# A two-layer graph network on one core: b2's row added by GpSimd, and the node matrix as one float32r product

## The chip, the cores and the metric

The kernel runs on one core of one Trainium2 chip. The metric is the device time of one execution in microseconds (us), the median over several runs. All times below are in microseconds unless marked ns. The engines are called by the profile's names: PE (TensorE, matrix products), DVE (VectorE), ACT (ScalarE), POOL (GpSimd), SP (SyncE, which issues most of the DMAs).

## What is computed

There are 128 independent graphs of 128 nodes with 512 features each, and a dense adjacency matrix per graph. The reference, cut down:

```python
h = relu(layernorm(x))
# layer 0: two hypergraph convolutions
def hypergraph_conv(x, adj, W, b):
    H = (adj != 0)
    w = adj[:, 0, :]                        # first row, weight of each hyperedge
    xw = einsum('ncd,hd->nch', x, W)
    Dn = 1 / einsum('nce,ne->nc', H, w)     # 0 where the sum is 0
    Be = 1 / H.sum(axis=1)
    m = Be[:, :, None] * einsum('nce,nch->neh', H, xw)
    return Dn[:, :, None] * einsum('nce,neh->nch', H, m) + b
t = relu(hypergraph_conv(h, adj, W1, b1))   # 512 -> 1024
t = layer_norm(t, gamma, beta)
x = x + hypergraph_conv(t, adj, W2, b2) + h # 1024 -> 512
# layer 1
h = relu(layernorm(x))
deg = adj.sum(-1)
agg = einsum('bij,bjf->bif', adj, h) / maximum(deg, 1e-6)
x = x + relu(concat([h, agg]) @ W.T)        # 1024 -> 512
```

The two products with H in one convolution are one matrix per graph, S = H diag(Be) H^T, and the sum for Dn is one more column beside it. That matrix is called the node matrix below.

## The kernel before

**Tiling.** One graph is one tile: 128 nodes on the 128 partitions, features along the free axis. All weights stay in SBUF. The products with weights are exact to float32 by a split: each operand is held as a high part, a low part and a third combination of both, all in float32r, and a product is high x high + low x low into one PSUM bank (names ending in m: rm, gm, bm, am) and the third parts into another (rd, gd, bd, ad). So a product of 128 x 512 by 512 x 512 is twelve matrix instructions of 512 columns. The helper `product` issues them; its lines in the profile are L489 (the m bank) and L494 (the d bank).

**Stages and order.** The program is written as small functions, one stage of one graph each, and the order in which they are called is the order of each engine's queue: nothing is reordered later. `step(s)` is called for s from 3 to 124 and holds one call of each stage, for graphs s-4 to s+3 (a software pipeline); `head()` loads and splits the weights and starts the first graphs, `tail()` finishes the last. `steady(g)` is true for graphs 3 to 120; for these conv2's node product (L701 to L703) is split too, and the sum of x, h and b2 is made differently (below).

**What the change touches.**

- `incidence(g)`: a transpose of the adjacency (adjt, L385), the weight column (L387), the test for non-zero with its count (L389), the count's floor and reciprocal (L391, L392), all on DVE. `incidence_scale` multiplies adjt by the reciprocal, on POOL in `step` (L303, tile sb).
- `node_matrix(g)`: one float32 product of adjt with the 129 columns of sb (L404, tile ps_s), and a copy by ACT to SBUF (L406, tile s). float32 products appear as two records each.
- `node_scale(g)`: five small DVE operations in a row on 128x1 tiles (L415 to L420, tile dinv).
- `mean_operator(g)`: a row sum, its floor and its reciprocal on DVE (L339 to L341, tile deg); `mean_scale` scales the adjacency by it, on ACT in `step` (L301).
- `residual(g)`: POOL adds h to x in two halves of 256 columns (L81, tile x_t); then, for steady graphs, `moved` adds b2's row with an accumulating DMA from SBUF to SBUF, issued by POOL (L91). For other graphs POOL adds it, in two more halves.
- `layer1_low(g)`: the low part of layer 1's transposed input (tile hl, L81), on DVE in `step`.
- `combine` splits what POOL does into halves of 256 columns; on DVE it is one instruction of full width. conv1_bias (tile r), conv2_bias (tile g) and residual (x_t) are POOL's additions in `step`.
- `shifts(s - 2, 3)`: a product of two 128x1 columns for a norm, on POOL in `step` (L303, tile st).

Two activations make round trips through DRAM for a transpose: n (inner_out, inner_in, inner_turn with the transpose L550 to nt) and h (layer1_trip_out, layer1_trip_in, layer1_turn, L550 to ht). The adjacency makes one too (mean_out, mean_in, mean_transpose). SP issues all of these.

Of the kernel before, what the change touches and what calls it, by code (L numbers as in the profile page):

```python
# [7 lines left out]
FP = mybir.dt.float32  # L8
FR = mybir.dt.float32r
# [15 lines left out]
def gnn_kernel(  # L25
# [64 lines left out]
    def moved(t, src):  # L90
        nc.gpsimd.dma_start(out=t, in_=src, accum_op=ADD)  # L91

# [66 lines left out]
    b1_bc = const.tile([P, DH], FP, name="b1_bc")  # L159
    b2_bc = const.tile([P, D], FP, name="b2_bc")  # L160
    c0 = const.tile([P, D], FP, name="c0")
# [130 lines left out]
    @stage  # L292
    def load_adjb(g, queue=nc.sync):
        ADJB[g] = pool.tile([P, P], FP, tag="adjb", name="adjb", bufs=2)
        load_blocks(ADJB[g], adj[g], queue)
# [36 lines left out]
    SB, HT, S, DN, H0, Z, PZ, SPLIT = ({} for _ in range(8))  # L332

    @stage
    def mean_operator(g):

        a = ADJ.pop(g)
        deg = small.tile([P, 1], FP, tag="deg", name="deg", bufs=2)
        nc.vector.tensor_reduce(deg, a, AX.X, ADD)  # L339
        nc.vector.tensor_scalar(deg, deg, EPS_DEG, 1.0 / 4096.0, MAX, MUL)  # L340
        nc.vector.reciprocal(deg, deg)  # L341
        ADJ[g] = a, deg
# [37 lines left out]
    @stage  # L380
    def incidence(g):


        HT[g] = at = pool.tile([P, P], FP, tag="ht", name="adjt")
        nc.vector.transpose(at, ADJB.pop(g))  # L385
        SB[g] = sb = small.tile([P, P + 1], FP, tag="sb", name="sb")
        nc.vector.tensor_scalar(sb[:, P : P + 1], at[:, 0:1], DOWN_12, None, MUL)  # L387
        cnt = small.tile([P, 1], FP, tag="cnt", name="cnt", bufs=2)
        nc.vector.tensor_scalar(at, at, 0.0, None, ALU.not_equal, ADD, accum_out=cnt)  # L389

        nc.vector.tensor_scalar(cnt, cnt, 1.0, None, MAX)  # L391
        nc.vector.reciprocal(cnt, cnt)  # L392
        SB[g] = sb, cnt

    @stage
    def incidence_scale(g, eng):
        SB[g], cnt = SB[g]
        scaled(eng, SB[g][:, :P], HT[g], cnt)


    @stage
    def node_matrix(g):
        ps = small_bank("ps_s")
        nc.tensor.matmul(ps[:, : P + 1], HT.pop(g), SB.pop(g), start=True, stop=True)  # L404
        s = small.tile([P, P + 1], FP, tag="s", name="s", bufs=4)
        copy(s, ps[:, : P + 1], AF.Copy, scale=4096.0 if steady(g) else 1.0)  # L406
        S[g] = s[:, :P]
# [3 lines left out]
    def node_scale(g):  # L411
        w = DN[g]
        DN[g] = dn = small.tile([P, 4], FP, tag="dinv", name="dinv", bufs=6)
        inv = dn[:, 2:3]
        nc.vector.tensor_scalar(inv, w, TINY, None, MAX)  # L415
        nc.vector.reciprocal(inv, inv)
        nc.vector.scalar_tensor_tensor(dn[:, 0:1], w, 0.0, inv, ALU.is_gt, MUL)
        nc.vector.tensor_scalar(dn[:, 1:2], dn[:, 0:1], ONE_UP, None, MUL)
        if not steady(g):
            nc.vector.tensor_scalar(dn[:, 3:4], dn[:, 0:1], DOWN_12, None, MUL)  # L420
# [15 lines left out]
    def residual(g, eng=nc.gpsimd):  # L436
        combine(eng, X[g], X[g], H0[g], ADD)
        if steady(g):
            moved(X[g], b2_bc)
        else:  # L440
            combine(eng, X[g], X[g], b2_bc, ADD)
# [373 lines left out]
    def step(s):  # L815
        node_high(s - 2)
        layer1_high(s - 3)
        conv2_bias(s - 2)
        inner_out(s - 1)
        inner_in(s - 1)  # L820
        conv2_high(s - 2)
        node_rest(s - 2)
        node_matrix(s + 1)
        mean_out(s - 3)
        layer1_low(s - 3, nc.vector)
        layer1_self_main(s - 4)
        conv1_weights(s, 1)
        mean_in(s - 3)
        conv2_low(s - 2, nc.vector)
        layer1_self_out(s - 4)  # L830
        conv2_rest(s - 2)
        conv2_nodes(s - 2)
        finish(s - 4)
        load_adj(s - 2)
        layer1_rest(s - 3)
        x_norm(s + 1)
        conv1_main(s, 0)
        conv2_out(s - 2)
        store(s - 4)
        conv1_nodes(s + 1)  # L840
        conv1_main(s, 1)
        conv1_out(s, 1)
        conv1_out(s, 0)
        conv1_high(s + 1)
        conv1_bias(s, 1)
        layer1_mean(s - 3)
        inner_turn(s - 1)
        layer1_sums(s - 2)
        conv1_bias(s, 0)
        conv1_low(s + 1)  # L850
        layer1_self(s - 3)
        layer1_mean_main(s - 3)
        layer1_spread(s - 2)
        load_adjb(s + 3)
        inner_high(s - 1)
        scales(s - 2, 3)
        mean_transpose(s - 3)
        shifts(s - 2, 3, nc.gpsimd)
        layer1_norm(s - 2)
        inner_sums(s)  # L860
        layer1_mean_out(s - 3)
        layer1_mean_high(s - 3)
        inner_low(s - 1, nc.vector)
        mean_rest(s - 3)
        inner_rest(s - 1)
        layer1_mean_low(s - 3, nc.vector)
        layer1_mean_rest(s - 3)
        inner_spread(s)
        scales(s, 2)
        shifts(s, 2, nc.gpsimd)  # L870
        conv2_weights(s - 1)
        layer1_trip_out(s - 2)
        residual(s + 1)
        incidence(s + 2)
        inner_norm(s)
        aggregate(s - 3)
        node_scale(s + 1)
        load_x(s + 2)
        mean_operator(s - 2)
        conv2_main(s - 1)  # L880
        layer1_trip_in(s - 2)
        conv2_weights_out(s - 1)
        x_sums(s + 2)
        x_spread(s + 2)
        mean_scale(s - 2, nc.scalar)
        conv1_rest(s + 1)
        layer1_turn(s - 2)
        incidence_scale(s + 2, nc.gpsimd)
        conv1_weights(s + 1, 0)
        scales(s + 2, 1)  # L890
        shifts(s + 2, 1, nc.vector)

    def head():
        load_w1(0, 0)
        load_x(0)
        load_adjb(0, nc.scalar)
# [547 lines left out]
```

## Time and profile before

| | |
|---|---|
| median of 3 runs | 2458.73 (2458.61 to 2459.32) |
| the profiled execution's own time | 2458.89 |
| its span in the trace | 2457.1 |
| PE busy | 2437.2 (99%) |
| DVE busy | 2340.8 (95%) |
| ACT busy | 2061.8 (84%) |
| POOL busy | 1016.1 (41%) |
| granted PE clock | 1.0 |
| mean DMA rate | 139 GB/s |
| moved by the accumulating DMAs (queue q0) | 30.95 MB in 118 issues, 7.2% of the 16 DMA engines |

Busy time is the union of the spans of an engine's instructions. PE's spans are modelled and overlap, so the cost of one product is read from the distance of two starts, not from its length. The same goes for DVE: an instruction of 0.69 in a row of others starts its follower after 0.61. Spans on POOL are rough. A group's "idle before" is the time in which its engine did nothing just ahead of it, with the one that ended it.

### The profile page before, as it was taken

The page shows a single profiled execution, that of the slowest core. Times are in us where ns is not written, and L with a number is a line of the kernel's source. Part 1 is how long each engine was busy: PE and PEld are TensorE (multiplying, and loading weights), DVE is VectorE, ACT ScalarE, POOL GpSimd, SP SyncE. Part 2 cuts the span into 40 slices and gives each one's busy share as a digit, 9 for nine tenths or more (in the row PEclk, how much of TensorE's full clock was granted, in tenths as well). Part 3 has the DMA queues.
Part 4 walks back from the last instruction along what each step waited for, and adds up shares of the span by engine and source line. Part 5 has one row for each costly group of instructions (what it writes and reads, how often), then busy time and mean ns, then how long its engine had stood idle before and what let it go on. Part 6 is the DMA issues. An engine that isn't in the chain of part 4 may idle for free.

```text
span 2457.1 us, 41143 instructions
## 1 busy us (share of the span) xinstructions
PE 2437.2 (99%) x11300; PEld 2023.8 (82%) x11300; DVE 2340.8 (95%) x5358; ACT 2061.8 (84%) x4494; POOL 1016.1 (41%) x1560
## 2 busy tenths in 40 slices
PE   8999999999999999999999999999999999999998
PEld 6788888888888888888888888888888888888886
DVE  8899999999999999999999999999999999999987
ACT  8888888888888888888888888888888888888885
POOL 5434343444344434443444434343434343434452
PEclk9999999999999999999999999999999999999999
DMA  7454554445444544454455444544554454445432
GB/s 193 132 139 136 141 143 139 136 142 146 136 137 140 149 135 138 139 150 132 139 144 145 136 138 142 143 136 138 144 141 137 138 146 139 136 138 145 127 121 94
DMA packets 425943, 342.30 MB, mean 139 GB/s; under 512 B 178544, under 2 KB 341872, under 8 KB 425712
## 3 DMA queue, kind: packets, MB, share of 16 engines
q1 hardware_dynamic: 407888, 308.66, 41.0%
q0 software_dynamic: 17248, 30.95, 7.2%
q8 instruction: 89, 1.46, 0.3%
q14 instruction: 142, 1.16, 0.2%
q10 hardware_dynamic: 576, 0.07, 0.0%
HBM read 166.21 MB, written 142.34 MB: 126 GB/s over the span
## 4 chain that ended last, share of the span: by engine, by line
PE 83%; DVE 12%; issue 2%; ACT 2%; DMA 1%; SPq 0%; POOL 0%; DVEq 0%; ACTq 0%; POOLq 0%
PE gm L489 16%; PE rm L489 16%; PE bm L489 8%; PE am L489 8%; PE gd L494 8%; PE rd L494 8%; PE bd L494 4%; PE ad L494 4%; PE pz L447 4%; PE am L791 2%; PE ad L791 1%; DVE r L514 1%; PE ps_s L404 1%; PE yd L703 1%; PE ym L701 1%
## 5 line engine op out<-in xcount | busy, mean ns | idle before, releaser
L81 POOL TENSOR_TENSOR r<-r,b_bc 128x256 f32<-128x256 f32 x500 | 355.5, 743 | 772.5 <-DVE r L514 481.4
L303 POOL TENSOR_SCALAR st<-st 128x1 f32<-128x1 f32 x252 | 76.1, 302 | 566.9 <-DVE st L320 566.9
L460 ACT ACTIVATE z<-pz 128x512 fp32r<-128x512 f32 x128 | 76.5, 598 | 206.3 <-PE pz L447 206.3
L329 ACT ACTIVATE r<-r,st 128x1024 f32<-128x1024 f32 x128 | 159.3, 1244 | 76.7 <-POOL st L303 76.6
L81 POOL TENSOR_TENSOR g<-g,c 128x256 f32<-128x256 f32 x246 | 211.1, 1019 | 3.8 <-DVE g L653 3.8
L329 ACT ACTIVATE h<-x_t,st 128x512 f32<-128x512 f32 x255 | 206.2, 809 | 1.1 <-DVE st L303 0.4
L81 POOL TENSOR_TENSOR x_t<-x_t,h 128x256 f32<-128x256 f32 x256 | 184.7, 742 | 5.8 <-ACT h L329 5.8
L314 ACT ACTIVATE h<-x_t,st 128x512 f32<-128x512 f32 x255 | 183.5, 720 | 4.1
L514 DVE SCALAR_TENSOR_TENSOR r<-rd,dinv,r 128x512 f32<-128x512 f32 x256 | 179.8, 742 | 3.7 <-ACT r L509 1.8
L309 ACT ACTIVATE h<-x_t 128x512 f32<-128x512 f32 x255 | 159.5, 626 | 8.4 <-DVE x_t L713 5.5
L509 ACT ACTIVATE r<-rm,dinv 128x512 f32<-128x512 f32 x256 | 162.2, 690 | 4.2 <-PE rm L489 4.1
L550 DVE STREAM_TRANSPOSE nt<-nb 128x1024 f32<-128x1024 f32 x127 | 156.8, 1235 | 2.5 <-DMA nb<-n_scratch 2.5
L580 DVE SCALAR_TENSOR_TENSOR nd<-nh,nl 128x1024 fp32r<-128x1024 f32 x127 | 154.8, 1219 | 0.0
L81 DVE TENSOR_TENSOR nl<-nt,nh 128x1024 fp32r<-128x1024 f32 x126 | 152.2, 1208 | 0.0
L489 PE MATMUL rm<-w11h,z 128*128 128x512 f32 x512 | 152.0, 418 | 0.0
L489 PE MATMUL bm<-w30h,hh 128*128 128x512 f32 x504 | 146.9, 413 | 0.1
L447 PEld LDWEIGHTS pz<-s,h 128*128 128x128 f32 x1024 | 134.4, 192 | 13.7 <-ACT s L406 1.8
L314 ACT ACTIVATE junk<-r,st 128x1024 bf16<-128x1024 f32 x128 | 145.1, 1134 | 0.1
L489 PE MATMUL rm<-w11l,z 128*128 128x512 f32 x512 | 138.2, 392 | 0.0
L494 PE MATMUL rd<-w11d,z 128*128 128x512 f32 x512 | 138.0, 391 | 0.0
L447 PE MATMUL pz<-s,h 128*128 128x128 f32 x1024 | 135.9, 276 | 1.9 <-ACT s L406 1.3
L489 PE MATMUL rm<-w10h,z 128*128 128x512 f32 x512 | 137.7, 391 | 0.0
(240 smaller groups left out, 7527.0 us busy)
## 6 DMA issues: line engine op xcount, KB each, us to landing
n_scratch<-r SPq DMA_DIRECT2D x128, 512.0 KB, 2.6
nb<-n_scratch SPq DMA_DIRECT2D x508, 128.0 KB, 2.8
x_t<-in_x_dram SPq DMA_DIRECT2D x128, 256.0 KB, 2.8
h_scratch<-h SPq DMA_DIRECT2D x127, 256.0 KB, 2.0
hb<-h_scratch SPq DMA_DIRECT2D x508, 64.0 KB, 2.0
out_dram<-o SPq DMA_DIRECT2D x127, 256.0 KB, 2.1
x_t<-b_bc POOLq DMA_DIRECT2D x118, 256.0 KB, 3.7
adj_t<-in_adj_dram SPq DMA_DIRECT2D x128, 64.0 KB, 2.0
```

Of the source, the lines that this page charges most:

```text
L81: eng.tensor_tensor(dst[:, s], a[:, s], b[:, s], op)
L309: copy(junk, src, func, accum_out=t[:, 0:1])
L314: copy(junk, src, AF.Square, bias=t[:, 1:2], accum_out=t[:, 2:3])
L329: copy(dst, src, func, bias=t[:, 5:6], scale=t[:, 4:5])
L447: nc.tensor.matmul(z[:, k * P : (k + 1) * P], H0[g][:, k * P : (k + 1) * P], S[g], start=True, stop=True)
L460: copy(h, pz, AF.Copy, scale=DOWN)
L489: nc.tensor.matmul(pm, left[i](k), right(i, k), start=(i == 0 and k == 0), stop=(i == 1 and k == kk - 1))
L494: nc.tensor.matmul(pd, left[2](k), right(2, k), start=(k == 0), stop=(k == kk - 1), skip_group_check=True)
L509: copy(R[g][:, HALVES[half]], PY.pop((g, half)), AF.Copy, scale=DN[g][:, 1:2])
L514: nc.vector.scalar_tensor_tensor(r, PR.pop((g, half)), dn[:, 0:1], r, MUL, ADD)
L550: nc.vector.transpose(nt.rearrange("p k (i b) -> p k i b", b=B), t.rearrange("p i k a -> p k i a"))
L580: nc.vector.scalar_tensor_tensor(t, h, 2.0**-12, low, MUL, SUB)
```

## The change

`moved` and the accumulating DMAs are gone: a new stage `residual_bias` adds b2's row on POOL, for all graphs. The scaled adjacency is split into high and low by splitting the two scalars alone (`incidence_high`), so that the node matrix is one float32r product of 258 columns, high part and low part side by side; `node_sum` adds the two halves on DVE after ACT has copied the first. The small operations of incidence, node_scale and mean_operator become stages of their own, and are called apart from each other. The order of `step`, `head` and `tail` is new. The diff, cut to its core:

```diff
-    def moved(t, src):
-        nc.gpsimd.dma_start(out=t, in_=src, accum_op=ADD)
...
-        ADJB[g] = pool.tile([P, P], FP, tag="adjb", name="adjb", bufs=2)
+        ADJB[g] = pool.tile([P, P], FP, tag="adjb", name="adjb")
...
     def mean_operator(g):
         nc.vector.tensor_reduce(deg, a, AX.X, ADD)
-        nc.vector.tensor_scalar(deg, deg, EPS_DEG, 1.0 / 4096.0, MAX, MUL)
-        nc.vector.reciprocal(deg, deg)
+    def mean_degree(g, eng):
+        eng.tensor_scalar(deg, deg, EPS_DEG, 1.0 / 4096.0, MAX, MUL)
+    def mean_inverse(g):
+        nc.vector.reciprocal(deg, deg)
...
     def incidence(g):
-        HT[g] = at = pool.tile([P, P], FP, tag="ht", name="adjt")
-        nc.vector.transpose(at, ADJB.pop(g))
-        SB[g] = sb = small.tile([P, P + 1], FP, tag="sb", name="sb")
-        nc.vector.tensor_scalar(sb[:, P : P + 1], at[:, 0:1], DOWN_12, None, MUL)
-        nc.vector.tensor_scalar(at, at, 0.0, None, ALU.not_equal, ADD, accum_out=cnt)
-        nc.vector.tensor_scalar(cnt, cnt, 1.0, None, MAX)
-        nc.vector.reciprocal(cnt, cnt)
+        raw = pool.tile([P, P], FP, tag="ant", name="raw")
+        nc.vector.transpose(raw, ADJB.pop(g))
+        HT[g] = at = pool.tile([P, P], FP, tag="ht", name="adjt").bitcast(FR)
+        two = small.tile([P, 2], FP, tag="cnt", name="cnt", bufs=2)
+        nc.vector.tensor_scalar(at, raw, 0.0, None, ALU.not_equal, ADD, accum_out=two[:, 1:2])
+    def incidence_weight(g, eng):
+        scaled(eng, two[:, 0:1], raw[:, 0:1], DOWN_12)
+    def incidence_count(g, eng):
+        eng.tensor_scalar(two[:, 1:2], two[:, 1:2], 1.0, None, MAX)
+    def incidence_inverse(g):
+        nc.vector.reciprocal(two[:, 1:2], two[:, 1:2])
+    def incidence_high(g):
+        t = small.tile([P, 2 * P + 4], FP, tag="sb", name="sb")
+        SB[g] = sb = t.bitcast(FR)
+        h, l = sb[:, P : 2 * P + 3 : P + 2], sb[:, 2 * P + 1 : 2 * P + 4 : 2]
+        copy(h, two, AF.Copy, scale=DOWN)
+        nc.vector.tensor_tensor(l, two, h, SUB)
+        SPLIT["sb", g] = t[:, 2 * P + 2 : 2 * P + 3], t[:, 2 * P + 3 : 2 * P + 4]
-    def incidence_scale(g, eng):
-        scaled(eng, SB[g][:, :P], HT[g], cnt)
+    def incidence_scale(g, i, eng):
+        scaled(eng, SB[g][:, i * (P + 1) : i * (P + 1) + P], HT[g], SPLIT["sb", g][i])
...
     def node_matrix(g):
-        nc.tensor.matmul(ps[:, : P + 1], HT.pop(g), SB.pop(g), start=True, stop=True)
+        nc.tensor.matmul(ps[:, : 2 * P + 2], HT.pop(g), SB.pop(g)[:, : 2 * P + 2], start=True, stop=True)
         copy(s, ps[:, : P + 1], AF.Copy, scale=4096.0 if steady(g) else 1.0)
+    def node_sum(g):
+        nc.vector.scalar_tensor_tensor(s, PS.pop(g)[:, P + 1 : 2 * P + 2], 4096.0 if steady(g) else 1.0, s, MUL, ADD)
-    def node_scale(g):
-        nc.vector.tensor_scalar(inv, w, TINY, None, MAX)
-        nc.vector.reciprocal(inv, inv)
-        nc.vector.scalar_tensor_tensor(dn[:, 0:1], w, 0.0, inv, ALU.is_gt, MUL)
-        nc.vector.tensor_scalar(dn[:, 1:2], dn[:, 0:1], ONE_UP, None, MUL)
+    def node_floor(g, eng):
+        eng.tensor_scalar(dn[:, 2:3], w, TINY, None, MAX)
+    def node_scale(g):
+        nc.vector.reciprocal(dn[:, 2:3], dn[:, 2:3])
+        nc.vector.scalar_tensor_tensor(dn[:, 0:1], w, 0.0, dn[:, 2:3], ALU.is_gt, MUL)
+    def node_up(g, eng):
+        scaled(eng, dn[:, 1:2], dn[:, 0:1], ONE_UP)
...
     def residual(g, eng=nc.gpsimd):
         combine(eng, X[g], X[g], H0[g], ADD)
-        if steady(g):
-            moved(X[g], b2_bc)
-        else:
-            combine(eng, X[g], X[g], b2_bc, ADD)
+    def residual_bias(g, eng=nc.gpsimd):
+        combine(eng, X[g], X[g], b2_bc, ADD)
```

The new step, in full, since its order is the order of the queues:

```python
def step(s):
    node_high(s - 2); conv2_bias(s - 2); conv2_high(s - 2); layer1_self_main(s - 4)
    layer1_high(s - 3); inner_out(s - 1); conv2_low(s - 2, nc.vector); x_norm(s + 1)
    node_rest(s - 2); conv1_main(s, 0); layer1_self_out(s - 4); conv2_rest(s - 2)
    node_matrix(s + 1); conv1_weights(s, 1); conv1_out(s, 0); mean_out(s - 3)
    layer1_low(s - 3); layer1_rest(s - 3); inner_in(s - 1); conv2_nodes(s - 2)
    node_sum(s + 1); node_floor(s + 1, nc.gpsimd); conv2_out(s - 2); conv1_main(s, 1)
    conv1_out(s, 1); inner_turn(s - 1); layer1_sums(s - 2); mean_in(s - 3)
    layer1_spread(s - 2); conv1_bias(s, 0); load_adj(s - 2); incidence(s + 2)
    layer1_mean(s - 3); incidence_weight(s + 2, nc.vector); scales(s - 2, 3); layer1_mean_main(s - 3)
    finish(s - 4); conv1_bias(s, 1); shifts(s - 2, 3, nc.vector); conv1_nodes(s + 1)
    store(s - 4); load_x(s + 2); inner_high(s - 1); conv1_high(s + 1)
    mean_transpose(s - 3); layer1_mean_out(s - 3); layer1_self(s - 3); mean_operator(s - 2)
    inner_low(s - 1, nc.vector); inner_rest(s - 1); layer1_norm(s - 2); inner_sums(s)
    layer1_mean_high(s - 3); inner_spread(s); conv2_weights(s - 1); layer1_mean_low(s - 3, nc.vector)
    node_scale(s + 1); mean_rest(s - 3); layer1_trip_out(s - 2); x_sums(s + 2)
    incidence_count(s + 2, nc.vector); mean_degree(s - 2, nc.vector); conv2_main(s - 1); scales(s, 2)
    layer1_mean_rest(s - 3); layer1_trip_in(s - 2); conv1_low(s + 1); incidence_inverse(s + 2)
    residual(s + 1); mean_inverse(s - 2); conv2_weights_out(s - 1); conv1_rest(s + 1)
    shifts(s, 2, nc.gpsimd); load_adjb(s + 3); inner_norm(s); incidence_high(s + 2)
    layer1_turn(s - 2); x_spread(s + 2); aggregate(s - 3); mean_scale(s - 2, nc.vector)
    incidence_scale(s + 2, 0, nc.vector); scales(s + 2, 1); conv1_weights(s + 1, 0)
    incidence_scale(s + 2, 1, nc.vector); shifts(s + 2, 1, nc.vector); residual_bias(s + 1); node_up(s + 1, nc.vector)
```

In `head` the weights' loads and splits come in another order: both high parts of w10 and both of w11 are called ahead of conv1_high(0), and incidence_high(0) after w10's; incidence_scale(0, 0) is on POOL.

## The prediction

> **What bounds the kernel now.** I read the page from the top. Busy shares first, then the chain that ended last, then who PE waited for.
>
> ```profile
> PE 2437.2 (99%) x11300; PEld 2023.8 (82%) x11300; DVE 2340.8 (95%) x5358; ACT 2061.8 (84%) x4494; POOL 1016.1 (41%) x1560
> ...
> PE 83%; DVE 12%; issue 2%; ACT 2%; DMA 1%; SPq 0%; POOL 0%; DVEq 0%; ACTq 0%; POOLq 0%
> ```
>
> PE carries the chain, DVE stands close behind. In the list of PE's waits the longest is one of 7.7 us in the start-up; all others together are under 8 us:
>
> ```profile
> PE ps_s L404 <- DVE sb L303: 7.7, 1, 7.7
> ```
>
> So outside the start-up the time is the PE list itself. One step of it, from PE's timeline (start, length, group):
>
> ```profile
> 1212.11 1.07 PE L494 MATMUL gd<-w21d,nd 128*128 128x512 f32 x4
> ...
> 1215.51 1.07 PE L494 MATMUL rd<-w10d,z 128*128 128x512 f32 x4
> 1216.42 0.38 PE L404 MATMUL ps_s<-sb,adjt 128*128 128x129 f32 x2
> 1216.56 1.18 PE L489 MATMUL rm<-w11h,z 128*128 128x512 f32 x4
> 1217.57 1.08 PE L489 MATMUL rm<-w11l,z 128*128 128x512 f32 x4
> ```
>
> The spans overlap, so starts are read. Four products take 0.907 (1216.42-1215.51), one 0.227. From ps_s to 1217.57 is 1.15; less 0.907, the node matrix costs 0.24. A step holds 78 products (17.68), the eight short pz (0.90 in the same way) and ps_s: 18.82; the next ps_s comes 18.86 later. Between 100 and 2350 us PE is busy 2249.7 of 2250: 119 such steps.
>
> DVE's list is as long: its 42 instructions of a step follow each other without a hole. But some of it is waiting inside an instruction:
>
> ```profile
> 1212.28 0.17 DVE L416 RECIPROCAL dinv<-dinv 128x1 f32<-128x1 f32 x1
> 1212.48 0.39 DVE L417 SCALAR_TENSOR_TENSOR dinv<-s,dinv 128x1 f32<-128x1 f32 x1
> 1212.90 0.15 DVE L418 TENSOR_SCALAR dinv<-dinv 128x1 f32<-128x1 f32 x1
> ...
> 1215.77 0.51 DVE L682 SCALAR_TENSOR_TENSOR sp<-sp,s 128x128 fp32r<-128x128 f32 x1
> ```
>
> L417 takes 0.16 elsewhere (in the start-up), L682's twin L683 0.28. Both stand beside an addition of GpSimd, and end as it ends (1212.85, 1216.12):
>
> ```profile
> 1211.42 1.43 POOL L81 TENSOR_TENSOR x_t<-x_t,h 128x256 f32<-128x256 f32 x2
> 1213.15 0.90 POOL L91 DMA_DIRECT2D x_t<-b_bc  x1 [0.30 <-DVE dinv L418]
> 1213.81 0.91 POOL L303 TENSOR_SCALAR sb<-adjt,cnt 128x128 f32<-128x128 f32 x1
> 1214.39 1.73 POOL L81 TENSOR_TENSOR g<-g,c 128x256 f32<-128x256 f32 x2
> ```
>
> **What the Trainium skill says.** (1) SBUF — State Buffer, "Who interferes with whom": a DVE instruction with two SBUF inputs, or in a two-port mode, and a GpSimd instruction that reads SBUF exclude each other; the later waits the whole instruction. The trace agrees: 0.23 at L417, 0.26 at L682. (2) VectorE: DVE Perf Modes, "What auto-detection actually checks": a one-source SBUF operation in float32 can take that two-port mode, so the moved scalings may block too; no view here shows that. (3) TensorE: Matmul & The Clock Gate, "Back-to-back issue gap": N/2.4+2.5 ns, 216 for 512 columns; the trace has 227, so 11 more. (4) DMA: Bandwidth & Descriptors, "Rules for kernel authors": an accumulating DMA must come from GpSimd; here the one such queue is q0, 7.2% of the DMA engines.
>
> **The change part by part, per step.**
> *PE.* One float32r product of 258 columns for two float32 records of 129. By rate (213 of the 227 ns are columns at 2.4 per ns) 258/2.4+13 = 0.121. Gain 0.24-0.12 = **0.12**. Bounds: 0.11 (the skill's formula) to 0.45, if the width were charged at the float32 rate (0.24 x 2); I take 0.12, since every float32r row shows one rate. 119 steps: -14.5 us.
> *DVE, start to start.* Gone: layer1_low (0.60, to POOL), the floor of dinv (0.17). Added: three 128x128 scalings, 0.287 long by the start-up's (9.03 0.29 DVE L303), 0.20 start to start: +0.60; one shift +0.13; node_sum, 129 columns from PSUM, worked out from L514[...]: +0.26; the small low part of incidence_high +0.08. Sum +0.30. Small operations that now stand apart from what they read: L416 to L417 takes 0.20 where an independent one takes 0.08; eight such pairs become three: -0.58. The two port waits above go (-0.49). New port waits, from laying out the new order: finish meets residual's first half on POOL (0.30), the low part meets conv2_bias's first half (0.18), layer1_rest waits for POOL's layer1_low (0.1). 18.86+0.30-0.58-0.49+0.58 = **18.67**, less the short waits on ACT that are in the 18.86 (L320 starts its follower after 0.17, where 0.08 is its own): 18.6. PE's new step is 18.74, so PE stays the bound, by about 0.1. Behind layer1_rest's wait stand node_sum and conv2_out; POOL's node_floor and ACT's layer1_sums wait for those, none of them on PE's path within the next 3 us.
> *POOL.* Off: DMA issue 0.65, scaling 0.6, one shift 0.24. On: residual_bias and layer1_low, four halves of 0.70, floor 0.24. 7.9 busy becomes 9.4 of 18.7. Queued behind its waits: node_floor waits for node_sum, and conv1_bias behind it; conv1_bias feeds inner_sums, which then has 3 us before its result is read. Hidden, since PE reads nothing from POOL within its step but the h low part, 1.6 us later.
> *ACT.* Loses mean_scale (0.29), gains a copy of two columns (0.11). Hidden.
> *DMA.* The accumulation (31 MB) goes. SP's list moves: load_adj, the store and load_x come ahead of the h trip, mean_in's four issues after inner_in's, load_adjb's four behind the h trip. They have room: the h trip leaves after layer1_norm, 2.5 to its first read (h_scratch issued 1207.65, hb 1210.18), four issues of 0.44, landing 2.0: 2.53+1.32+2.0 = 5.9 after norm's end, against 6.8 in the laid-out order (7.15 before: 1207.64 to 1214.79) until the transpose reads it. One buffer for adjb instead of two costs nothing: its reader is some ten us away on both sides.
> *The new wait.* sb was scaled on POOL, 1.7 us ahead of ps_s; now it is DVE's last large work. From the start of the last gd product PE needs 16 x 0.227 = 3.63 to ps_s's slot. DVE from there: the product's span and the waking of g 0.39+0.09, g 0.61, z 0.59, wait for POOL's half 0.17, low part 0.08, ht 0.63, three scalings and a reciprocal 0.20+0.20+0.08+0.29, handing over 0.06: **3.39**. In time, by 0.24, of which the weight load ahead of the product wants 0.1 to 0.2. Queued behind the low part on DVE are ht, the scalings, the shift of x and gp; ACT waits for ht, PE for the scalings. If that cover goes, ps_s and all PE work behind it, the w11 products first, is late by as much in every step.
> *Start-up.* PE's first ps_s starts at 9.37 and its first rm at 13.64, and it idles in most of the time until then. In the new order incidence_high(0) stands on ACT behind both w10 high parts (1.05 each, the second half landed at 8.6) and is scaled on POOL in 0.91 instead of on DVE in 0.29: ps_s near 11.5. node_sum(0) stands on DVE behind w10's second low part and its rest (1.2 each): pz near 13.5 instead of 10.88. conv1_high(0) stands on ACT behind two w11 high parts (1.0 each): first rm near 17.5. That is +4, and PE has no slack later to win it back; bounds 2 (if the loads land as before and the queues overlap better) and 7 (if w2's loads, now ahead of x's third, delay more): **+4.5**. The other nine node matrices and the end: 0 ± 2. Late h or adjacency landings, now felt at ps_s: +1.
> Sum -14.5+4.5+1 = **-9** on the profiled execution's 2458.89 (span 2457.1), which is 0.2 over the median: 2449.7.
>
> **Rivals.**
> *A, ps_s comes late by a little.* For: the cover is 0.24 less the load. Against: nothing on DVE ahead of it is unmeasured but the low part and the second and third scaling. 0.1 late gives back 12 us: 2462; from 0.075 on the change is no gain.
> *B, DVE is shut out for a whole GpSimd pair: slower.* For: it happened before,
>
> ```profile
> 1102.56 1.21 DVE L682 SCALAR_TENSOR_TENSOR sp<-sp,s 128x128 fp32r<-128x128 f32 x1
> ```
>
> while both halves of g ran. Place: low part and finish, in every step. Price: 0.70 more ahead of ps_s, 0.46 late, less 0.12: +0.34 x 119 + 5.5 = +46: 2505. Against: those g halves follow a DMA issue and a long scaling and start 0.34 before the first ends; other pairs start 0.04 before, and there DVE gets in between:
>
> ```profile
> 30.28 0.30 DVE L417 SCALAR_TENSOR_TENSOR dinv<-s,dinv 128x1 f32<-128x1 f32 x1
> ```
>
> beside pairs begun at 29.09 and 30.53. The change takes DMA and scaling off POOL's steady list. It decides from 0.2 more at the low part.
> *C, 258 columns at the float32 rate:* +0.21 x 119 + 5.5: 2489. Against: the one rate of 512.
> *D, the gain is there and the start-up eats it:* 2455 to 2460.
>
> **How the numbers follow.** Likeliest 0.66 at 2449.7, own range 2443 to 2454 (rate bound, start-up 2 to 7). A 0.18, some of it still faster, the rest across zero; B 0.06; C 0.03; D 0.07. A measurement here tells about 0.2% (4.9 us) from no change. Faster 0.67, same 0.18, slower 0.15. The range takes in the likeliest, D and most of A: 2442 to 2468.
>
> **What would show it.** ps_s one record of 258 columns, about 0.12 to the next start, a step of 18.74; PE's waits without ps_s outside the start-up; no L682-like stretch on DVE, one short one at finish and at the low part; first rm near 17 us. Wrong if ps_s waits for DVE in each step, if the scalings take over 0.35, or if the step is not 18.7 to 18.8.

## The result and the profile after

The changed kernel takes **2447.64 us** (median of 5 runs, 2447.03 to 2449.41) against 2458.73 for the kernel before on the same chip: ratio 0.9955, 95% interval 0.9941 to 0.997. The forecast was 2449.7. The profiled execution took 2447.67, with a span of 2445.9. In what follows, an interval behind a median is that of its ratio to the kernel before, measured beside it. The experiments ran on several chips, where the kernel before took 2458.4 to 2459.0, so a difference from the changed kernel is good to about 0.6 us.

The page of the changed kernel: busy time by engine, and the engines' shares of the chain that ended last.

```profile
PE 2422.7 (99%) x11170; PEld 2009.6 (82%) x11170; DVE 2298.1 (94%) x5843; ACT 2009.9 (82%) x4512; POOL 1324.8 (54%) x1808
...
PE 95%; ACT 2%; DVE 1%; DMA 1%; issue 1%; SPq 0%; POOL 0%; POOLq 0%; DVEq 0%; ACTq 0%
```

PE has 14.5 us less to do (2437.2 before). The chain, which before went through DVE for 12%, now is PE's for 95%. POOL is 309 us busier, 10.3 a step where 9.4 was forecast, and nothing shows it on the chain.

What PE waited for (us in total, times, longest):

```profile
PE ps_s L430 <- ACT sb L298: 11.4, 1, 11.4
PE py L738 <- DVE g L81: 2.1, 2, 1.1
...
PE ps_s L430 <- DVE sb L300: 0.3, 1, 0.3
PE ps_s L430 <- DVE st L300: 0.2, 1, 0.2
```

```profile
PEld ps_s L430 <- ACT gp L706: 2.3, 7, 0.5
```

The 11.4 is the very start. After that PE waits 0.5 us in all for ps_s, whose operand now comes from DVE's last large work; its weight load (PEld) waits another 2.3 us in seven steps, five of them among the few longer ones (below). PE's timeline of a step (start, length, group):

```profile
1212.13 0.28 PE L430 MATMUL ps_s<-sb,adjt 128*128 128x258 f32 x1
1212.25 1.09 PE L530 MATMUL rm<-w11h,z 128*128 128x512 f32 x4
1213.18 1.09 PE L530 MATMUL rm<-w11l,z 128*128 128x512 f32 x4
...
1230.88 0.28 PE L430 MATMUL ps_s<-sb,adjt 128*128 128x258 f32 x1
```

One record instead of two, and 0.12 to the next start (0.120 over 69 steps). The next ps_s comes 18.75 later. The median distance of two steps is 18.747, against 18.860 before.

DVE's timeline, around the three places where the prediction saw it at risk:

```profile
1219.68 1.04 DVE L844 SCALAR_TENSOR_TENSOR o<-o,x_t 128x512 f32<-128x512 f32 x1
...
1226.97 0.14 DVE L347 RECIPROCAL deg<-deg 128x1 f32<-128x1 f32 x1
1227.74 0.69 DVE L694 SCALAR_TENSOR_TENSOR g<-gd,g 128x512 f32<-128x512 f32 x1 [0.62 <-issue]
1228.35 0.68 DVE L508 SCALAR_TENSOR_TENSOR z<-z,pz 128x512 fp32r<-128x512 f32 x1
1228.94 0.33 DVE L419 TENSOR_TENSOR sb<-cnt,sb 128x2 fp32r<-128x2 f32 x1
...
1230.25 0.27 DVE L300 TENSOR_SCALAR sb<-adjt,sb 128x128 fp32r<-128x128 f32 x1
```

Beside them, POOL's two pairs and PE's last four gd products:

```profile
1219.43 1.90 POOL L81 TENSOR_TENSOR x_t<-x_t,h 128x256 f32<-128x256 f32 x2
1228.51 1.44 POOL L81 TENSOR_TENSOR g<-g,c 128x256 f32<-128x256 f32 x2 [0.56 <-DVE g L694]
```

```profile
1226.58 1.07 PE L535 MATMUL gd<-w21d,nd 128*128 128x512 f32 x4
```

finish (L844) takes 1.04 where 0.68 is its own, the low part (L419) 0.33 where 0.15 is: these are the two waits for GpSimd. And DVE now stands idle 0.62 ahead of g (L694), because PE's gd bank isn't finished: its last product ends at 1227.65, g starts at 1227.74 (the profile puts the wait down to "issue"). DVE is early. From L694's start the last scaling of sb ends after 2.78 (1230.52), and PE's slot for it comes 0.36 later.

### The profile page after: what moved, and what is told of

Read it like the earlier page. It is cut to its first block, busy times and chain, and to the rows that moved or that the text cites. A ratio compares the mean times of both kernels' runs of the same rounds, so it can differ in the third digit from the quotient of the medians.

```text
span 2445.9 us, 41647 instructions
## 1 busy us (share of the span) xinstructions
PE 2422.7 (99%) x11170; PEld 2009.6 (82%) x11170; DVE 2298.1 (94%) x5843; ACT 2009.9 (82%) x4512; POOL 1324.8 (54%) x1808
## 4 chain that ended last, share of the span: by engine, by line
PE 95%; ACT 2%; DVE 1%; DMA 1%; issue 1%; SPq 0%; POOL 0%; POOLq 0%; DVEq 0%; ACTq 0%
PE gm L530 19%; PE rm L530 18%; PE am L530 9%; PE bm L530 9%; PE gd L535 9%; PE rd L535 9%; PE bd L535 5%; PE ad L535 5%; PE pz L488 4%; PE am L832 2%; PE ad L832 1%; PE ym L743 1%; PE yd L744 1%; PE ym L742 1%; PE ps_s L430 1%
## 5 line engine op out<-in xcount | busy, mean ns | idle before, releaser
L300 POOL TENSOR_SCALAR st<-st 128x1 f32<-128x1 f32 x130 | 82.3, 633 | 569.9 <-DVE st L317 563.2
L81 POOL TENSOR_TENSOR hl<-ht,hh 128x256 fp32r<-128x256 f32 x250 | 235.4, 963 | 216.5 <-ACT hh L612 216.5
L81 POOL TENSOR_TENSOR x_t<-x_t,h 128x256 f32<-128x256 f32 x256 | 239.8, 959 | 1.3 <-ACT h L326 1.1
L81 POOL TENSOR_TENSOR g<-g,c 128x256 f32<-128x256 f32 x246 | 177.6, 743 | 72.4 <-DVE g L694 72.4
L555 DVE SCALAR_TENSOR_TENSOR r<-rd,dinv,r 128x512 f32<-128x512 f32 x256 | 190.8, 746 | 7.7 <-ACT r L550 6.3
L81 POOL TENSOR_TENSOR x_t<-x_t,b_bc 128x256 f32<-128x256 f32 x256 | 187.2, 752 | 0.0
L550 ACT ACTIVATE r<-rm,dinv 128x512 f32<-128x512 f32 x256 | 174.7, 684 | 7.7 <-PE rm L530 4.4
L694 DVE SCALAR_TENSOR_TENSOR g<-gd,g 128x512 f32<-128x512 f32 x127 | 87.8, 691 | 79.5 <-issue 70.4
L530 PE MATMUL am<-w31h,hh 128*128 128x512 f32 x504 | 146.8, 413 | 0.0
L530 PE MATMUL rm<-w11h,z 128*128 128x512 f32 x512 | 140.3, 396 | 0.0
```

The lines of the kernel that those rows point to most:

```text
L81: eng.tensor_tensor(dst[:, s], a[:, s], b[:, s], op)
L530: nc.tensor.matmul(pm, left[i](k), right(i, k), start=(i == 0 and k == 0), stop=(i == 1 and k == kk - 1))
L550: copy(R[g][:, HALVES[half]], PY.pop((g, half)), AF.Copy, scale=DN[g][:, 1:2])
L555: nc.vector.scalar_tensor_tensor(r, PR.pop((g, half)), dn[:, 0:1], r, MUL, ADD)
L694: nc.vector.scalar_tensor_tensor(G[g], PG.pop(g), 4096.0, G[g], MUL, ADD)
```

## Experiments

### The product alone undone, in the new order

```diff
-        nc.tensor.matmul(ps[:, : 2 * P + 2], HT.pop(g), SB.pop(g)[:, : 2 * P + 2], start=True, stop=True)
+        nc.tensor.matmul(ps[:, : P + 1], HT.pop(g), SB.pop(g), start=True, stop=True)
...
-        nc.vector.scalar_tensor_tensor(s, PS.pop(g)[:, P + 1 : 2 * P + 2], 4096.0 if steady(g) else 1.0, s, MUL, ADD)
```

> The changed kernel with the node matrix as one float32 product of 129 columns again, everything else in the new order: incidence_high copies the weight column only, one scaling on DVE instead of two, no node_sum. Theory (PE's list sets the step, and the product's 0.12 is the whole gain): ps_s is two records again and costs 0.24, the step goes from 18.75 to 18.87, 128 node matrices x 0.115 = +14.7, so about 2462 (2459 to 2465), although DVE has 0.6 us less to do in each step. Rival (the gain comes from the new order, from the two waits on GpSimd that are gone on DVE): the time stays at 2446 to 2450, or falls, since DVE has less work.

Measured: 2461.28 (1.0004 to 1.002). The step is 18.860 again, +0.113; against the changed kernel +13.6. DVE had less to do and that bought nothing. So PE's list sets the step in the new order, and the product is what the change gains: without it the new order is 2.5 us slower than the old one.

### The accumulating DMA: put back in the new order, taken out of the old one

```diff
-        combine(eng, X[g], X[g], b2_bc, ADD)
+        if steady(g):
+            nc.gpsimd.dma_start(out=X[g], in_=b2_bc, accum_op=ADD)
+        else:
+            combine(eng, X[g], X[g], b2_bc, ADD)
```

> The changed kernel with b2's row added by an accumulating DMA again for the steady graphs, at the place of residual_bias. Theory (the DMA and its replacement are both off the path): 31 MB more on the DMA engines, POOL 0.5 to 0.7 less busy in each step, step 18.75, time 2447.6 +- 1.5. Rival 1 (the removal of the transfers is part of the gain; loads land later with them): 2450 to 2458, with more idle time of DVE before ht and nt. Rival 2 (a GpSimd DMA ahead of the pair on g shuts DVE out for both halves): the low part of sb takes 1.0 instead of 0.33 and the time is 2490 or more.

Measured: 2465.79 (1.0018 to 1.0041), 18 us more than the changed kernel. The theory missed; rival 1 had the direction and too little. Most steps are 18.75 as before, but 15 of 117 are longer, thirteen of these by 1.0 to 1.6, together 16.7 us. PE's and DVE's waits name the chain:

```profile
PE ps_s L430 <- DVE st L300: 13.4, 13, 1.4
...
DVE ht L594 <- DMA hb<-h_scratch: 16.0, 14, 1.7
```

One such step in SP's, POOL's and DVE's timelines. The first line is the issue of hb one step earlier, the second that of the late step:

```profile
458.48 1.75 SPq L587 DMA_DIRECT2D hb<-h_scratch  x4
...
477.22 3.06 SPq L587 DMA_DIRECT2D hb<-h_scratch  x4
```

```profile
478.82 0.88 POOL L483 DMA_DIRECT2D x_t<-b_bc  x1
```

```profile
483.03 0.71 DVE L594 STREAM_TRANSPOSE ht<-hb 128x512 f32<-128x512 f32 x1 [1.46 <-DMA hb<-h_scratch]
```

Here SP's four issues took 3.06 instead of 1.75, so that the last ended at 480.28, and the transpose came 2.75 behind that. But the long issue alone isn't the cause. The changed kernel has nine such issues (the one at 474.48 took 3.01 for four). There the last block of hb lands 1.5 behind the last issue's end (2.1 once), and DVE is late by 0.54 at most in the steady part. And of the thirteen late steps only seven have a long issue; in the other six, h landed in DRAM 3.2 to 3.6 behind its issue instead of 2.4, and hb's issues, of the usual length, started about 1 us late.

What the thirteen share is the accumulating transfer: it is issued 0.9 to 1.5 ahead of the end of hb's last issue, and that block then lands 2.6 to 3.0 behind the end. In 101 of the other steps it is issued less than 0.5 ahead, and the median is 1.56; one step in between, at 0.82, has 1.70. The trace's DMA packets show what happens. Those of one transfer (queue q0) take about 1.3 us, and in that time q1, the queue of SP's transfers, moves 5 KB per us in the median step, where its average in the changed kernel is 123. In the step shown, from 480.50 to 481.75, q0 moves 200 KB and q1 35; when q0 is done, q1 moves 73 KB in 0.25 us (from 482.00). The loads of adjb, which SP issues next in every step, feel it too: 2.5 us from issue to landing in the median, 1.7 in the changed kernel.

So a block of hb that is still under way when the transfer begins waits for it. Why q1 all but stops, and doesn't share, no run here shows.

The other way round, in the kernel before:

```diff
-        if steady(g):
-            moved(X[g], b2_bc)
-        else:
-            combine(eng, X[g], X[g], b2_bc, ADD)
+        combine(eng, X[g], X[g], b2_bc, ADD)
```

> The kernel before with the accumulating DMA alone replaced: GpSimd adds b2's row in two more halves of 256 columns, in the place of the DMA's issue. Theory (in the old order the trip of h has room, and the transfers cost nothing there): step 18.86, 2458.7 +- 3. Rival 1 (the transfers delay others in any order): 1 to 16 us less, since a late trip of hb costs nothing any more. Rival 2 (DVE's list was full, so GpSimd's 0.7 us more before the pair on g moves or lengthens DVE's waits): 0.1 to 0.5 more in each step, 2470 to 2520.

Measured: 2457.53 (0.9988 to 1.0005): no change, as the theory had it. The transfers cost nothing in the old order, and 18 us in the new one. In the old order they are issued 2.97 behind hb's first issue, as a rule after its last; in the new one 1.60 behind it, before the last has ended.

### The same work on DVE in two places

Ahead of g, three repeats of mean_rest's last operation; behind g, three repeats of sb's first scaling:

```diff
-            nc.vector.scalar_tensor_tensor(d, h, -4097.0, full, MUL, ADD)
+            for _ in range(4 if steady(g) else 1):
+                nc.vector.scalar_tensor_tensor(d, h, -4097.0, full, MUL, ADD)
```

> The changed kernel with three more DVE instructions in each steady step, repeats of the 128x128 scalar_tensor_tensor of mean_rest that write the same values again (0.202 each, 0.61 together), ahead of DVE's wait for PE's gd bank. Theory (DVE has 0.66 us to spare there in each step, g L694 is what it waits for): the wait before g shrinks from 0.66 to about 0.06, step 18.75, time 2447.6 +- 2. Rival (DVE's list is as long as PE's, as its 94% busy time says, with no more than 0.1 to spare): 0.5 x 119 = +60, 2508.

```diff
-        scaled(eng, SB[g][:, i * (P + 1) : i * (P + 1) + P], HT[g], c)
+        for _ in range(4 if steady(g) and i == 0 else 1):
+            scaled(eng, SB[g][:, i * (P + 1) : i * (P + 1) + P], HT[g], c)
```

> The changed kernel with three more DVE instructions in each steady step, repeats of the first 128x128 scaling of sb that write the same values again (0.196 each, 0.59 together), between g and the last scaling of sb: the same amount as in the other kernel, placed 3 us later. Theory (from the start of the last gd product to the last scaling's end DVE takes 3.28 and PE's slot for ps_s comes 3.63 after it; 0.35 to spare, of which 0.1 to 0.2 go to the weight load): ps_s is 0.35 to 0.45 late in every step, step 19.1 to 19.2, time +42 to +54: 2490 to 2502, and PE waits for DVE at ps_s in each step. Rival (a wait of PE there is taken up by the 0.66 that DVE has ahead of the next g): 2447 to 2450.

Measured: 2485.61 ahead of g (1.0093 to 1.0121), 2553.03 behind it (1.0373 to 1.0401). Both exceed the theory's figure, for one reason: the dose was larger than planned. A repeat that writes the same columns as its predecessor starts 0.31 to 0.33 behind it, not 0.20. DVE's timelines, first ahead of g, then behind it:

```profile
1204.56 1.26 DVE L378 SCALAR_TENSOR_TENSOR anp<-anp,ant 128x128 fp32r<-128x128 f32 x4
...
1207.25 0.67 DVE L695 SCALAR_TENSOR_TENSOR g<-gd,g 128x512 f32<-128x512 f32 x1
```

```profile
1207.33 1.25 DVE L300 TENSOR_SCALAR sb<-adjt,sb 128x128 fp32r<-128x128 f32 x4
```

So 0.98 was added ahead of g and 0.97 behind it. Ahead of g the wait is gone, and 0.98 less the 0.66 to spare is 0.32; the period over 69 steps is 19.07 to 19.08, 0.32 more. 117 x 0.32 = 37, and 38 were measured. Behind g, 0.97 less a cover of 0.21 (below) is 0.76, plus 0.08 because ps_s costs 0.196 to the next start when PE has to stop for it, instead of 0.120: 0.84; the median step rose by 0.82. Over 117 steps that is 96 us; of the rest, 5 are lost by the first steady ym and 4 in a few longer steps. One amount of work costs 38 us in one place and 105 in another, 3 us later on the same engine. The rival of a list with no slack (0.5 x 119 = +60 for a dose of 0.61) is out: at the larger dose it would have given over 100 ahead of g.

The cover itself: in both of these kernels, and in the next one, ps_s starts 0.146 after the recorded end of the last scaling whenever PE waits for it. In the changed kernel it starts 0.353 after it on average (0.364 in the median step). So 0.353 - 0.146 = 0.21 is to spare.

### GpSimd's pair on g as one instruction

```diff
-        combine(eng, G[g], G[g], c0, ADD)
+        if steady(g):
+            nc.gpsimd.tensor_tensor(G[g], G[g], c0, ADD)
```

> The changed kernel with conv2_bias on POOL as one instruction of 512 columns instead of two halves of 256, for the steady graphs. Theory (the low part of sb waits for the GpSimd instruction that runs when it comes; a half holds it 0.18): it now waits for the end of the whole, some 0.7 more, so the low part takes about 1.0 instead of 0.33, the last scaling of sb is 0.7 later against 0.35 of cover with the weight load in it, ps_s is 0.45 to 0.55 late, time +54 to +65: 2501 to 2513. This is the mechanism of rival B. Rival (DVE gets in between in any case, or has room for it): 2446 to 2450.

Measured: 2495.45 (1.0132 to 1.0163), +47.8 on the changed kernel, a little under the theory. POOL's, DVE's and PE's timelines:

```profile
1213.37 1.30 POOL L699 TENSOR_TENSOR g<-g,c 128x512 f32<-128x512 f32 x1 [0.46 <-DVE g L694]
```

```profile
1213.80 0.89 DVE L419 TENSOR_TENSOR sb<-cnt,sb 128x2 fp32r<-128x2 f32 x1
```

```profile
1216.08 0.36 PE L430 MATMUL ps_s<-sb,adjt 128*128 128x258 f32 x1 [0.18 <-DVE st L300]
```

An operation on two columns takes 0.89, since it waits until GpSimd is done (1214.67 and 1214.69). That is 0.56 more than in the changed kernel; less 0.21 of cover, plus 0.08, would be 0.43, and the step rose by 0.39. This is rival B's mechanism and nearly its price. What keeps the changed kernel from it is the split into halves.

### The small operations back in rows

```diff
         incidence(s + 2)
+        incidence_count(s + 2, nc.vector)
+        incidence_inverse(s + 2)
...
         mean_operator(s - 2)
+        mean_degree(s - 2, nc.vector)
+        mean_inverse(s - 2)
...
+        node_floor(s + 1, nc.vector)
         node_scale(s + 1)
+        node_up(s + 1, nc.vector)
```

> The changed kernel with the small DVE operations of a step back in rows: incidence_count and incidence_inverse right behind incidence, mean_degree and mean_inverse right behind mean_operator, node_floor on DVE ahead of node_scale and node_up behind it. Theory (an operation that reads the one before it costs 0.12 more, start to start): six new pairs, 0.72, and the floor's 0.07 make DVE's list 18.09 + 0.79 = 18.88 against PE's 18.75: DVE's wait before g is gone and the step is 18.8 to 18.9, +5 to +16 us: 2452 to 2464. Rival (0.66 to spare hides them): 2446 to 2449.

Measured: 2463.78 (1.0012 to 1.0025), +16.1, the upper end of the theory. Each link costs what was said: the count starts 0.33 behind the test that it reads, its reciprocal 0.19 behind it.

```profile
1209.75 0.29 DVE L393 TENSOR_SCALAR_CACHE_REDUCE adjt<-raw 128x128 fp32r<-128x128 f32 x1
1209.96 0.08 DVE L393 DVE_READ_ACCUMULATOR adjt<-raw 128x1 f32 x1
1210.08 0.15 DVE L405 TENSOR_SCALAR cnt<-cnt 128x1 f32<-128x1 f32 x1
1210.27 0.16 DVE L410 RECIPROCAL cnt<-cnt 128x1 f32<-128x1 f32 x1
...
1210.47 0.67 DVE L844 SCALAR_TENSOR_TENSOR o<-o,x_t 128x512 f32<-128x512 f32 x1
```

But the step isn't evenly longer: its median stays 18.75, 36 of 117 steps are 0.1 to 0.9 longer, together 17 us, and DVE still waits ahead of g in 52 steps. That the mean, 18.89, meets the forecast list of 18.88 is luck, since such a list would lengthen every step. The theory overlooked that finish (L844) no longer meets GpSimd in most steps: over 69 steps its follower starts 0.62 behind it, 0.95 in the changed kernel. So DVE's list stays under PE's (0.79 less 0.32 is less than the 0.66 to spare), and what is lost is most of its room. Of the 36 longer steps, DVE waits for hb ahead of the transpose in 12 and for ACT ahead of r in 10 others; the remaining 14 aren't explained. Over the whole run:

```profile
DVE r L555 <- ACT r L550: 10.4, 15, 1.8
DVE ht L591 <- DMA hb<-h_scratch: 8.0, 13, 1.4
```

In the changed kernel these two are 6.3 in 8 and 3.1 in 4. So setting the small work apart is worth 16 us here, and not as time of its own: it is the room in which DVE takes up such waits.

### The product alone, in the old order

The float32r product with its two scalings on DVE and node_sum, in the order of the kernel before, with one adjacency buffer, as in the changed kernel. Here incidence_scale holds incidence_high's two instructions and both scalings.

```diff
-        ADJB[g] = pool.tile([P, P], FP, tag="adjb", name="adjb", bufs=2)
+        ADJB[g] = pool.tile([P, P], FP, tag="adjb", name="adjb")
...
         layer1_rest(s - 3)
+        node_sum(s + 1)
...
-        load_adjb(s + 3)
...
         incidence(s + 2)
+        load_adjb(s + 3)
...
-        incidence_scale(s + 2, nc.gpsimd)
+        incidence_scale(s + 2, nc.vector)
```

> The kernel before with the float32r product of 258 columns alone: incidence_high's two instructions, two scalings on DVE in the place of POOL's one, and node_sum behind layer1_rest; b2 still by the accumulating DMA, the small operations in rows, the order as before but for the adjacency block's load, which stands behind incidence since it has one buffer now. Theory (DVE's list was as long as PE's): DVE gets 0.26 + 0.08 + 0.40 = 0.74 more, less some of the 0.49 of its waits for GpSimd since POOL's long scaling is gone; step 19.1 to 19.6, time +30 to +85 on the kernel before: 2490 to 2543. So the product alone makes it slower, and the new order is what lets PE keep the 0.12. Rival (DVE's full list was only waiting): step 18.75, 2444 to 2450.

Measured: 3085.13 (1.2532 to 1.2566), far outside either. It tested something else (PE's granted clock, too, was 0.93 here). SP, whose queue is in order, waits for the single buffer until DVE has transposed out of it, and the trip of h is queued behind:

```profile
SPq L277 <- DVE raw L386: 413.7, 125, 3.6
```

The load was moved so that this wait vanishes:

```diff
         layer1_spread(s - 2)
+        load_adjb(s + 2)
...
         incidence(s + 2)
-        load_adjb(s + 3)
```

> The kernel before with the float32r product of 258 columns alone, as in the run before, but with the load of an adjacency block kept in its old place in SP's queue and one graph later (its single buffer is free by then), so that SP isn't held behind DVE: in the run before SP waited 414 us for it and everything behind it came late. Theory (DVE's list was as long as PE's): DVE gets 0.74 us more in each step (node_sum 0.26, low part 0.08, two scalings 0.40), less what goes of its 0.49 of waits for GpSimd; step 19.1 to 19.6: 2490 to 2543, slower than the kernel before. Rival (the full list of DVE was waiting that would give way): 2444 to 2450.

Measured: 2584.58 (1.05 to 1.0529), +126 on the kernel before; the direction is the theory's, the amount beyond it. The step is 19.77, and PE's largest wait is new:

```profile
PE pz L460 <- DVE s L419: 92.4, 120, 2.8
```

node_sum stands in DVE's list behind everything that was there, pz needs its result, and 0.77 of PE's time goes in each step. DVE itself idles some 0.46 a step waiting for ACT (31.9 and 23.0 us in two waits), so its own work is near 19.3. It isn't shown how much a better place for node_sum would bring in the old order; with the placement tried, a step loses 0.91 us where the product alone would give 0.11.

### The start-up

Three other starts. First the small chain of graph 0 ahead of the weight splits, and no filling products:

```diff
-        w1[0].low(0)
         incidence_high(0)
+        incidence_scale(0, 0, nc.vector)
+        incidence_scale(0, 1, nc.vector)
...
-        fill(768)
...
+        w1[0].rest(0, nc.vector)
+        incidence(1)
```

> The changed kernel with another start: both scalings of graph 0's sb and its shift on DVE ahead of w10's low parts, conv1_high, low and rest of graph 0 ahead of the second w11 high part and of w10's rest, and no filling products of 768 columns. Theory (PE's start-up waits for a chain of small operations that stand behind weight splits): first ps_s near 10.5 instead of 11.4, first rm near 14.5 instead of 16.9; DVE has the same work to do in the start-up, so only part of it reaches the first steady step: 0.5 to 2 us less, 2445.6 to 2447.1. Rival (DVE's weight splits set the start-up): first rm earlier, but the first ym product at 108.1 as before, 2447.6.

Then the order of the changed kernel with three edits, the fill moved ahead of the node matrix:

```diff
-        w1[0].rest(1, nc.vector)
...
-        shifts(0, 1, nc.gpsimd)
+        shifts(0, 1, nc.scalar)
...
+        fill(2560)
         node_matrix(0)
-        fill(768)
         w1[1].high(1)
...
+        w1[0].rest(0, nc.vector)
...
+        conv1_high(0)
         w1[1].high(0)
...
-        w1[0].rest(0, nc.vector)
+        conv1_low(0)
+        conv1_rest(0)
+        w1[0].rest(1, nc.vector)
...
-        conv1_high(0)
-        conv1_low(0)
-        conv1_rest(0)
```

> The changed kernel with its start altered in three places only: filling products of 2560 columns ahead of the first node matrix (while PE has nothing else to do) instead of 768 behind it, graph 0's shift on ACT instead of POOL, and conv1_high, low and rest of graph 0 ahead of the second w11 high part and of w10's second rest. Theory (in the other start PE's first twelve conv1 products took 0.47 each after two pauses, and graph 1's incidence came late): first rm near 14.5 at 0.25 to 0.3 each, first ym at 106.5 to 107.6, time 2446 to 2447. Rival (DVE's weight splits set the start-up): first ym at 108.1 or later, 2447.6 or more.

Then the same with PE kept at work until its operands are there:

```diff
-        fill(2560)
+        fill(4608)
         node_matrix(0)
+        fill(512)
```

> The changed kernel with the start of the run before (head2), but with filling products of 4608 columns ahead of the first node matrix, so that PE works without a break until its operands are there (about 11.1), and 512 columns behind it. Theory (after a break PE's products take twice as long, 427 ns instead of 227 for 512 columns, for about 4 us; in head2 that fell on the first eight rm and cost 1.6 us): the first eight rm take 0.23 to 0.24 each, first rm near 15, first ym 1 to 1.6 us earlier than in head2: 107.3 to 107.9, time 2446.5 to 2449. Rival (the start-up is set by DVE, and PE's speed there is free): rm at 0.23 each too, but first ym at 108.5 or later, 2449.5 to 2451.

| | first rm | first ym | median | ratio to before |
|---|---|---|---|---|
| before | 13.64 | 106.6 | 2458.73 | |
| changed | 16.88 | 108.1 | 2447.64 | 0.9941 to 0.997 |
| head | 15.34 | 113.9 | 2454.18 | 0.9974 to 0.999 |
| head2 | 15.33 | 108.9 | 2450.67 | 0.9956 to 0.9981 |
| head3 | 14.43 | 108.3 | 2448.53 | 0.9945 to 0.9972 |

head lost 6 us where 0.5 to 2 were to be won: graph 1's incidence had come to stand behind w10's rest on DVE (ps_s of graph 1 at 21.9 instead of 19.8), and PE's first products ran at half speed. head2 lost 3 us where about 1 was to be won. The first four rm, in the changed kernel, head2 and head3:

```profile
16.88 1.20 PE L530 MATMUL rm<-w10h,z 128*128 128x512 f32 x4 [0.94 <-ACT z L501]
```

```profile
15.33 2.07 PE L530 MATMUL rm<-w10h,z 128*128 128x512 f32 x4 [0.69 <-ACT z L501]
```

```profile
14.43 1.20 PE L530 MATMUL rm<-w10h,z 128*128 128x512 f32 x4 [0.69 <-ACT z L501]
```

In head2 PE had been idle for 3.25 us ahead of ps_s, and its products take 427 ns each until 19.3, 227 after that; in head3, without the pause, they take 0.23 from the second on. The Trainium skill has this (TensorE: Matmul & The Clock Gate, "Part 1: The HAM clock gate"): half the clock until the array has been busy for about 3.4 us. The runs agree: head2's granted clock is 0.50 from 12.5 to 19.3 and 1.00 behind that, after 4 us of rm without a pause; head3's is 1.00 from 5.5 on.

So head3's first rm comes 2.4 us ahead of the changed kernel's, as its theory wanted. But its first ym comes at 108.3, which neither the theory (107.3 to 107.9) nor the rival (108.5 or later) had, and not ahead of 108.1 at all: PE's start isn't what sets the start-up. By 21.2 the w11 products start at the same time in both. What does set it stays open. None of the three beats the changed kernel (head3's runs, 2447.58 to 2448.94, overlap with its own), and no other run points to a version that would.

## Why the prediction was right

- **PE.** 0.12 per step, 14.5 in all: 0.113 between the step medians, 14.5 between the pages' busy times, 13.6 when the product alone is undone. Rival C, the float32 rate, is out at the first record.
- **DVE's list.** Right that it wouldn't bind, wrong in size: 18.6 was forecast, "by about 0.1" under PE; 18.09 is there, 0.66 under it (shown by the dose ahead of g). The pieces that were priced came in close: scalings 0.16, 0.20 and 0.18 for 0.20, the shift 0.12 for 0.13, node_sum 0.20 for 0.26, the wait in the low part 0.18 for 0.18, at finish 0.34 for 0.30, none at layer1_rest for 0.10. The term that was mis-sized is the last one, the "short waits on ACT in the 18.86", taken at 0.07: over 69 steps bl took 0.80 to its follower before and takes 0.61 now, and two of the norms' short reciprocals took 0.16 and 0.17 where 0.07 is left, 0.37 together, 0.30 more than was priced. Nor was most of it waiting for ACT. In the trace of the kernel before, bd, right behind bl, and the shift, right behind its reciprocal, wait for DVE's own semaphore: two more pairs that the new order sets apart, where the prediction had seen waits on ACT. With the 0.10 at layer1_rest and 0.12 on the scalings and node_sum, less 0.04 at finish, this is nearly all of the 0.51. The margin forecast, 0.1, was thin; that 0.66 came of it is owed to what was mis-sized, and that much is luck.
- **The new wait.** From the last gd product DVE was given 3.39, 0.06 of it for handing over; it takes 3.28 to the scaling's recorded end, and handing over with the weight load takes 0.146. Spare: 0.21 where 0.24 less 0.1 to 0.2 was forecast. Rival A is out for the changed kernel, though the dose behind g shows it is real from 0.21 on.
- **Rival B** is out for the halves, and g_whole shows its mechanism at 0.39 a step.
- **DMA, costed at nothing.** Half right. The accumulation costs nothing in the old order. In the new one it would have cost 18 us, in the steps where hb is late and the transfer comes in ahead of its last block. The prediction's own margin, 5.9 against 6.8, fits the usual step (landed 1.5 behind the last issue, read 2.55 behind it); it didn't ask about the late one. What was left, late landings, was forecast at +1: 1.5 in five steps of 117 (in four of them the transpose waits for hb), against 0.8 in two before, so 0.7 more.
- **Start-up, +4.5.** The steps were near: ps_s 11.40 for 11.5, pz 14.3 for 13.5, first rm 16.88 for 17.5. What failed is "PE has no slack later to win it back": of 3.2 us at the first rm, 1.5 is left at the first steady ym. Between the two PE stands idle for 2.55 us where it was 3.29 before, and the node matrices save some 0.6 there; the rest fits the first rm of the kernel before, which ran at half the clock until 14.4. In the sum, +1.5 at the first ym, -12.5 over 117 steps and -0.2 at the end make -11.2. Against the forecast the start-up is 3.0 us better, the steps (-14.5 and +1 were forecast) 1.0 worse: two errors that in part cancel make the 2.1 us between forecast and result. Rival D, the gain eaten by the start-up, is out.

## What to carry to other kernels

Where two engines' lists are equally full, find out which one waits for the other before costing an edit: the same 0.98 us on DVE cost 0.32 a step ahead of its wait for PE and 0.82 behind it. A transfer or a single buffer that is free in one order of the queues can cost tens or hundreds of us in another, so it has to be costed in the step where its neighbour is late, not in the usual one. And a start-up is measured where the steady part begins, not at its first product.

## What the runs showed of the hardware

- A DVE operation of 128x128 that writes the columns its predecessor wrote starts 0.31 to 0.33 behind it instead of 0.20, though it reads nothing of them. In the trace such a repeat has a wait for DVE's own semaphore and starts 0.035 after its predecessor's recorded end; mean_rest's two operations, which write different columns of one tile, have none and start 0.20 apart. So the 0.12 of a dependent pair is the price of that wait, whether for a read or for a write. What DVE would do without it no run shows.
- While the packets of an accumulating transfer of 256 KB run, about 1.3 us, the queue of SP's transfers moves 5 KB per us (median of accum_dma), and a block of hb under way then lands 1.0 to 1.4 later.
- A DVE operation that meets GpSimd's work on the pair of additions to g waits for the instruction that runs: 0.18 with two halves of 256 columns, 0.74 with one of 512.
- A float32r product of 258 columns costs 0.120 in a running stream and 0.196 when PE has waited for its operand.
- SP's DMA issues take 0.43, but 47 of them in the changed kernel took 0.9 to 2.0; eight of hb's nine came 300 us apart, that is every 16 steps. No run here shows why.
